# Masks ahead of sums, statistics in other slots, and the last decodes on VectorE, in a pre-norm graph-attention kernel

## The chip, the cores and the metric

The kernel runs on one core of a Trainium2 chip. A core has five engines that run at the same time, each working through its own queue in order: TensorE (PE in the profile; its weight loads are listed apart as PEld) multiplies matrices into PSUM, VectorE (DVE), ScalarE (ACT) and GpSimd (POOL) work element by element, and SyncE (SP) issues the transfers between memory and the on-chip SBUF. In this kernel POOL works from SBUF to SBUF only. An engine waits on semaphores that other engines raise, and whatever stands behind a waiting instruction in the same queue waits too.

The metric is the time of one execution in device microseconds; less is better. The median of three runs of the kernel before is 2755.74 us (2753.53 to 2756.32).

## The reference

The input x has 128 graphs of 128 nodes with 768 features, and adj has a 128 x 128 matrix for each graph. All is float32. For every graph:

```python
h = maximum(layernorm(x), 0)
q, k, v = (split_heads(h @ W + b) for W, b in ((Wq, bq), (Wk, bk), (Wv, bv)))   # 12 heads of 64
scores = q @ k.T / sqrt(64) + beta * adj
scores = where(adj > 0, scores, -9e15)
out = x + merge_heads(softmax(scores) @ v)
```

The three projections (768 x 768 each) are most of the arithmetic.

## The kernel before

**Groups and slices.** The 128 graphs go in 32 groups (G = 0 to 31) of 4. A group's projections are three slices: `qk0` (queries and keys of heads 0 to 5), `v` (all values) and `qk1` (queries and keys of heads 6 to 11). Each slice multiplies a 512 x 768 block of activations by weights. Group 0 does this plainly (`plain_slice`) and meanwhile VectorE and POOL prepare sums of weight blocks (`prepare`, lines 281 to 304), which are stored to memory. From group 1 on a fast scheme takes 15 block products in place of 18 (table `PRODUCTS`), and each block product is again split, into 7 small ones in place of 8. Both need sums: of activations, made by VectorE once per group (`sum_acts`, line 454, names S0 to S14) and by POOL (`inner`, lines 459 to 461), and of weights, streamed in again for every group through a ring of five buffers (`load_T`, line 335), except for eleven that stay in SBUF.

**Slots.** A slice from group 1 on is 15 slots, numbered 0 to 14, in the order that the tables `ZORDER` (qk0 and v), `QORDER` (qk1) or `LORDER` (qk1 of the last group) give. One slot is one product: 14 matmuls on line 537 into a PSUM bank pair, then work on the other engines. `run` and `behind_product` emit each slot in this order: the matmuls and the load of a later weight tile; then the steps listed for the slot; then the masks pending from earlier scores; then whatever has fallen due (`overdue`); then the copies of the product out of PSUM; then the queued exponentials and divisions (`trail`); and last the steps listed as "post" of the slot. Since each engine works in order, this is the order in every engine's queue. `then(at, f, ...)` puts a step in a slot, `then((at, "post"), f, ...)` behind it.

**Copies and decodes.** A product belongs to one of four chains (a, b, c, d). The first product of a chain takes a bank pair, further ones add to it, and the last gives it back. After each product the parts are added to their place: ScalarE copies where it is the first for that place (lines 552, 555, 557), VectorE adds otherwise (line 561). When a place has all its parts, `decode` turns the seven sums into queries and keys (lines 577 to 580) or values (588 to 592), one slot later or as `LAG` says, on POOL; only the decode behind product 13 of `qk1` is on VectorE. There are four bank pairs. From slot 2 to slot 9 of `qk0` the chains a, b and c hold three, and one is left for scores and attention.

**Attention.** For each pair of heads `scores` (line 614) multiplies keys and queries into a bank pair, `mask` (line 622, VectorE) adds the adjacency bias, writes to SBUF and gives the bank back, ScalarE takes the exponential (line 624), `attend` multiplies with the values (line 671, interleaved with the next product), ScalarE copies the result out (lines 680, 682) and divides (line 654) and VectorE adds x (line 696). The scores of `qk1`'s heads come in the next group's `qk0`, in slots 3, 5 and behind slot 6, so that their masks fall in slots 4, 6 and 7, and their attention behind slots 7, 10 and 12. In the last slice of the last group half steps are used (`scores_half`, lines 719 and 724; `attend_half`, lines 740 to 767).

**Statistics.** The layer normalisation of a later group is prepared by row: `load_row` (line 402) loads one graph's 128 x 768 block into the one place `row_home`, and `row_stats` (lines 409 to 411, ScalarE) takes its sum and its squared deviations, three instructions and two accumulator reads. As there is one place, the load of the next graph waits in SP's queue until the statistics before it are done. `row_moments` (line 416, then POOL 421 and 422, then two small transfers on lines 427 and 428) turns four graphs' statistics into the block layout in which `norm` (line 438, ScalarE) applies them to x, loaded by `load_x` (line 189). `to_hT` (line 449) transposes. In groups G with `G + 2 < NG` (NG = 32, so up to group 29) the statistics are those of group G + 2; group 1 does in addition those of group 2, as the fast scheme begins there.

Since group 30 has no group two after it, it runs `qk0` without statistics.

Of the kernel before, what the change touches and what calls it, by code (L numbers as in the profile page):

```python
# [125 lines left out]
def direct(ctx, tc, x, adj, wq, bq, wk, bk, wv, bv, beta, out, bad):  # L126
# [196 lines left out]
    def order_of(G, sl):  # L323
        return LORDER if G == NG - 1 and sl == "qk1" else ORDER[sl]
# [163 lines left out]
    def later(f, slots=1):  # L488
        while len(deferred) < slots:
            deferred.append([])  # L490
        deferred[slots - 1].append(f)
# [29 lines left out]
    def product_z(G, sl, n):  # L521

        an, bn, chain, uses = PRODUCTS[n]
        mine = [i for i in order_of(G, sl) if PRODUCTS[i][2] == chain]
        first = n == mine[0]
        if first:
            banks[chain] = take()
        p = banks[chain].rearrange("p i (z w) -> p (i z) w", w=P)
        a = full[G, an]
        streamed = (sl, n) not in resident  # L530
        b = tz.pop((G, sl, n)) if streamed else resident[sl, n]
        for at, z in enumerate(ZONES):
            lhs, rhs = a[:, LEFT[z]], b[:, RIGHT[z]]
            if sl != "v":
                lhs, rhs = rhs, lhs
            for q in range(0, P, HD):
                nc.tensor.matmul(p[q:q + HD, at, :], lhs[:, q:q + HD], rhs, start=(first and at % 4 == 0),  # L537
                                 stop=True, skip_group_check=True)
            turn()
        if streamed:  # L540
            load_T()
        yield
        for (r, j), sign in uses:
            key = (G, sl, r, j)
            op = ALU.add if sign > 0 else ALU.subtract
            if key not in qk:
                left[key] = sum(k == (r, j) for q in PRODUCTS for k, _ in q[3])
                t = qk[key] = home_qk(*key, zones=True)
                if sl == "v":
                    bias = bv_b[:, j * 2 * P:(j + 1) * 2 * P].rearrange("p (i n) -> p i n", i=2)  # L550
                    nc.vector.tensor_tensor(t[:, 5:7], bias, p[:, 5:7], op)
                    nc.scalar.activation(t[:, 0:5], p[:, 0:5], AF.Copy, scale=float(sign))
                else:
                    oc = j + 3 * int(sl[2])
                    nc.scalar.activation(t[:, 0:5], p[:, 0:5], AF.Copy, scale=float(sign))  # L555
                    for at, of in ((5, 0), (6, 2)):
                        nc.scalar.activation(t[:, at], p[:, at], AF.Identity, bias=bqk[:, of, oc:oc + 1],  # L557
                                             scale=float(sign))
            else:
                t = qk[key]  # L560
                nc.vector.tensor_tensor(t, t, p[:, 0:7], op)  # L561
            left[key] -= 1
            if not left[key]:
                later(lambda r=r, j=j: decode(G, sl, r, j, nc.vector if (sl, n) == ("qk1", 13) else nc.gpsimd), 1 if order_of(G, sl) is LORDER else LAG.get((sl, n), 1))
        if n == mine[-1]:
            give(banks.pop(chain))
        yield
# [205 lines left out]

    def behind_product(at, todo):
        pending = [masking.popleft() for _ in range(len(masking))]
        for f in todo.get(at, ()):
            f()
        for f in pending:
            f()
        while weighing:  # L780
            weighing.popleft()()
        overdue()
# [256 lines left out]
    for G in range(1, NG):  # L1039
# [6 lines left out]
        if G == 1:  # L1046
            sums_at(1, ((0, "S6"), (1, "S7"), (2, "S0"), (5, "S5"), (7, "S14"), (9, "S11")))
            then((0, "post"), load_x, 2, 0)
            for g, at in enumerate((2, 6, 10, 14)):
                then((at, "post"), row_stats, 2, g)  # L1050
                if g < 3:
                    then((at, "post"), load_row, 2, g + 1)
        else:
            sums_at(G, ((0, "S7"), (1, "S0"), (4, "S5"), (7, "S14"), (9, "S11")))
            if more:
                for g in range(2):
                    for h in range(2):
                        then((2 * g + h, "post"), norm, G + 1, g, 2 * h, 2 * h + 2)
                turn_act(G + 1, ((8, "A01"), (9, "A00"), (11, "A02")), None)
                then((12, "post"), load_x, G + 1, 1)  # L1060
                if G + 2 < NG:
                    then((8, "post"), row_stats, G + 2, 0)
                    then((9, "post"), load_row, G + 2, 1)
        slice_z(G, "qk0", todo)

# [4 lines left out]
        if more:  # L1070
            then((11, "post"), add_raw, G + 1)
            if G == 1:
                then(1, row_moments, 2, 3, 4)
                for n, at in enumerate((6, 7, 8, 9)):
                    then((at, "post"), norm, 2, n // 2, n % 2 * 2, n % 2 * 2 + 2)
                turn_act(2, ((10, "A01"), (11, "A00"), (12, "A02")), 1)
                then((12, "post"), load_x, 2, 1)
            else:
                for n, at in enumerate((3, 4, 7, 8)):
                    then((at, "post"), norm, G + 1, 2 + n // 2, n % 2 * 2, n % 2 * 2 + 2)  # L1080
                turn_act(G + 1, ((10, "A11"),), 1)
                for at, name in ((4, "A01"), (5, "A00"), (6, "A02")):
                    then(at, inner, G + 1, name)
            if G + 2 < NG:
                if G == 1:
                    then((1, "post"), load_row, 3, 0)
                for g, at in ((0, 5), (1, 11)) if G == 1 else ((1, 1), (2, 5), (3, 10)):
                    then((at, "post"), row_stats, G + 2, g)
                    if g < 3:
                        then((at + 1, "post"), load_row, G + 2, g + 1)  # L1090
        slice_z(G, "v", todo)

        todo.clear()
# [2 lines left out]
        attention(G, 0, ((3, 2), (9, 1)))  # L1096
        attention(G, 0, ((12, 0),), 6)
        if G == 1:
            for n, at in enumerate((0, 1, 2, 3)):
                then((at, "post"), norm, 2, 2 + n // 2, n % 2 * 2, n % 2 * 2 + 2)  # L1100
            turn_act(2, ((4, "A10"), (5, "A11"), (6, "A12")), 1)
            then((5, "post"), row_stats, 3, 2)
            then((5, "post"), load_row, 3, 3)
            then((9, "post"), row_stats, 3, 3)
        else:
            turn_act(G + 1, ((1, "A10"), (4, "A12")), 1)
        sums_at(G + 1, ((6 + (G == 1), "S1"), (7 + (G == 1), "S9"), (8 + (G == 1), "S2"), (11, "S6"), (13, "S10")))
        bias(G + 1, 0, 2, 4)
        if G + 2 < NG:
            then(*((10, row_moments, G + 2, 3, 5) if G == 1 else (5, row_moments, G + 2, 6, 9)))  # L1110
            then((6, "post"), load_x, G + 2, 0)
        if G + 3 < NG:
            then((10, "post"), load_row, G + 3, 0)
        slice_z(G, "qk1", todo)
# [151 lines left out]
```

## Time and profile before

| | |
|---|---|
| median of 3 runs | 2755.74 us (2753.53 to 2756.32) |
| profiled execution | 2751.8 us, its span 2749.9 us |
| mean granted clock of TensorE | 0.997 |
| one steady group (1339.20 to 1422.50) | 83.3 us: PE busy 81.75, DVE 67.86, ACT 55.79, POOL 65.81 |
| memory traffic in that group | 267 GB/s, the DMA engines busy 0.88 of the time |

The rows of the order of time show start, length, engine, line, operation, tiles written and read, and in brackets the idle time of that engine just before, with what ended it. Matmul ends are modelled, so a busy TensorE is not a TensorE at its peak. A row of the list of waits reads: who waited, for whom, microseconds in total, times, longest. "issue" is time in which an engine waited for nothing that the profile shows.

### The profile page before, as it was taken

What the parts mean: (1) busy time and instruction counts of PE and PEld (TensorE: products, weight loads), DVE (VectorE), ACT (ScalarE), POOL (GpSimd) and SP (SyncE); (2) the same over time, 40 slices, a digit from 0 to 9 for tenths busy, and PEclk for the clock granted to TensorE, in tenths of its full rate; (3) what the DMA queues carried; (4) which work ended last, traced back from release to release, by engine and by line L of the source; (5) the groups of instructions that cost most, each with busy time, mean ns of one, the idle gap of its engine ahead of it and who ended that gap; (6) DMA issues with size and microseconds to landing.
All of it is one profiled execution on the core that took longest, in us unless ns stands there. A gap on an engine that the chain in (4) does not pass through costs nothing.

```text
span 2749.9 us, 121542 instructions
## 1 busy us (share of the span) xinstructions
PE 2671.3 (97%) x52029; PEld 2565.2 (93%) x52029; DVE 2194.7 (80%) x2693; ACT 1763.8 (64%) x4612; POOL 2107.5 (77%) x3046
## 2 busy tenths in 40 slices
PE   9999999999999999999999999999999999999997
PEld 7688999999999999999999999999999999999997
DVE  6867887788887788887788887778877888877885
ACT  1377666666666766666676666766667666667653
POOL 4757878777788778787778787777887787877784
PEclk9999999999999999999999999999999999999999
DMA  8788889898889898898898898988888988998875
GB/s 209 246 269 266 269 263 280 252 280 268 266 274 272 254 277 266 270 274 265 270 271 266 264 282 252 279 268 263 273 272 259 275 265 271 273 262 272 254 235 153
DMA packets 530342, 721.73 MB, mean 262 GB/s; under 512 B 105980, under 2 KB 374024, under 8 KB 529800
## 3 DMA queue, kind: packets, MB, share of 16 engines
q1 hardware_dynamic: 528640, 713.12, 85.5%
q8 instruction: 412, 6.75, 1.0%
q10 hardware_dynamic: 1160, 0.79, 0.1%
q14 instruction: 130, 1.06, 0.1%
HBM read 647.73 MB, written 66.05 MB: 260 GB/s over the span
## 4 chain that ended last, share of the span: by engine, by line
PE 61%; DVE 16%; DMA 6%; ACT 6%; POOL 5%; issue 3%; SPq 0%; DVEq 0%; POOLq 0%; ACTq 0%
PE pair L537 51%; PE pair L614 5%; DVE home L561 5%; PE pair L671 5%; DVE sbig L454 5%; DMA turned<-row 2%; DMA T_qk<-kept_qk 2%; DVE e L622 2%; DVE xo L696 2%; ACT sbig L411 1%; ACT sbig L409 1%; DMA sbig<-in_x_dram 1%; DVE sbig L561 1%; ACT home L555 1%; ACT home L557 1%
## 5 line engine op out<-in xcount | busy, mean ns | idle before, releaser
L561 DVE TENSOR_TENSOR home<-home,pair 128x896 f32<-128x896 f32 x810 | 861.0, 1076 | 284.7 <-PE pair L537 187.2
L537 PE MATMUL pair<-sbig,T_qk 128*64 128x128 f32 x13888 | 886.1, 274 | 3.3 <-ACT home L557 2.2
L537 PEld LDWEIGHTS pair<-sbig,T_qk 128*64 128x64 f32 x13888 | 754.7, 137 | 16.8 <-ACT home L557 7.6
L654 ACT ACTIVATE e<-e,sm 128x64 f32<-128x64 f32 x1512 | 382.2, 342 | 108.2 <-DVE sm L642 108.0
L671 PE MATMUL pair<-v,e 128*64 128x65 f32 x6048 | 401.5, 222 | 27.4 <-ACT home L557 18.6
L577 POOL TENSOR_TENSOR home<-home 128x256 f32<-128x256 f32 x299 | 228.8, 765 | 259.1 <-DVE home L561 249.5
L537 PE MATMUL pair<-A,T_qk 128*64 128x128 f32 x6076 | 414.6, 273 | 0.0
L537 PE MATMUL pair<-T_v,sbig 128*64 128x128 f32 x6944 | 412.3, 273 | 0.0
L555 ACT ACTIVATE home<-pair 128x640 f32<-128x640 f32 x325 | 228.6, 703 | 263.5 <-PE pair L537 202.9
L671 PEld LDWEIGHTS pair<-v,e 128*64 128x64 f32 x6048 | 356.0, 137 | 38.6 <-ACT home L557 24.1
L537 PEld LDWEIGHTS pair<-T_v,sbig 128*64 128x64 f32 x6944 | 383.7, 137 | 5.5 <-issue 5.2
L537 PEld LDWEIGHTS pair<-A,T_qk 128*64 128x64 f32 x6076 | 330.1, 137 | 5.5 <-issue 5.5
L580 POOL TENSOR_TENSOR home<-home 128x256 f32<-128x256 f32 x299 | 280.3, 938 | 23.5
L622 DVE SCALAR_TENSOR_TENSOR e<-pair,biasT 128x1024 f32<-128x1024 f32 x189 | 230.5, 1220 | 35.4 <-PE pair L614 35.4
L578 POOL TENSOR_TENSOR home<-home 128x256 f32<-128x256 f32 x299 | 238.5, 798 | 23.4
L680 ACT ACTIVATE sm<-pair,tiny 128x8 f32<-128x8 f32 x189 | 50.4, 267 | 312.0 <-PE pair L671 311.9
L624 ACT ACTIVATE e<-e 128x1024 f32<-128x1024 f32 x189 | 200.1, 1059 | 64.6 <-DVE e L622 47.9
L579 POOL TENSOR_TENSOR home<-home 128x128 f32<-128x128 f32 x299 | 216.4, 724 | 23.4
L438 ACT ACTIVATE x<-x,block 128x192 f32<-128x192 f32 x480 | 231.2, 538 | 4.4 <-DMA block<-turned 3.0
L537 PE MATMUL pair<-sbig,res_qk 128*64 128x128 f32 x3472 | 211.6, 273 | 0.5 <-DVE home L561 0.5
L614 PE MATMUL pair<-home 64*64 64x128 f32 x5312 | 187.8, 275 | 18.1 <-DVE e L622 18.1
L557 ACT ACTIVATE home<-pair,bqk 128x128 f32<-128x128 f32 x650 | 203.3, 373 | 0.0
(188 smaller groups left out, 4702.9 us busy)
## 6 DMA issues: line engine op xcount, KB each, us to landing
T_qk<-kept_qk SPq DMA_DIRECT2D x713, 448.0 KB, 4.8
T_v<-kept_v SPq DMA_DIRECT2D x341, 448.0 KB, 4.3
xo<-in_x_dram SPq DMA_DIRECT2D x189, 256.0 KB, 4.9
out_dram<-xo SPq DMA_DIRECT2D x189, 256.0 KB, 5.9
x<-in_x_dram SPq DMA_DIRECT2D x248, 192.0 KB, 6.2
sbig<-in_x_dram SPq DMA_DIRECT2D x120, 384.0 KB, 6.5
kept_qk<-prep_qk SPq DMA_DIRECT2D x23, 448.0 KB, 3.2
adj<-in_adj_dram SPq DMA_DIRECT2D x128, 64.0 KB, 3.4
```

Of the source, the lines that this page charges most:

```text
L438: nc.scalar.activation(t, t, AF.Relu, bias=shift[G, n], scale=rstd[G, n])
L537: nc.tensor.matmul(p[q:q + HD, at, :], lhs[:, q:q + HD], rhs, start=(first and at % 4 == 0), stop=True, skip_group_check=True)
L555: nc.scalar.activation(t[:, 0:5], p[:, 0:5], AF.Copy, scale=float(sign))
L557: nc.scalar.activation(t[:, at], p[:, at], AF.Identity, bias=bqk[:, of, oc:oc + 1], scale=float(sign))
L561: nc.vector.tensor_tensor(t, t, p[:, 0:7], op)
L577: e.tensor_tensor(t[:, 1:4:2], t[:, 1:4:2], twice(5), ALU.add)
L578: e.tensor_tensor(t[:, 2:5:2], t[:, 2:5:2], twice(1), ALU.add)
L580: e.tensor_tensor(t[:, 0:7:6], t[:, 0:7:6], twice(2), ALU.add)
L614: nc.tensor.matmul(ps[k:k + HD, i, g * N:(g + 1) * N], keys[r, k:k + HD], queries[r], start=True, stop=True)
L622: nc.vector.scalar_tensor_tensor(e, ps, SCORE_CAP * ISCALE, bias, op0=ALU.min, op1=ALU.add)
L654: nc.scalar.activation(o[:, r, b, 0:HD], pa[:, r, b, 0:HD], AF.Copy, scale=t[:, 1, r, b:b + 1])
L671: nc.tensor.matmul(pa[q:q + HD, 2 * g + i, :], k[:, q:q + HD], vt[G, "v", r, h // 4][:, 4 * g + h % 4, :], start=True, stop=True, skip_gro ...
```

## The change

Four edits:

1. `behind_product` runs the pending masks ahead of the slot's steps instead of behind them. Where a slot has both, the mask comes before the sums, transposes or weight sums of that slot in VectorE's queue. In `qk0` of the steady groups this is slot 4 (S5) and slot 7 (S14).
2. From group 2 on the statistics of the first row of group G + 2 move from behind slot 8 to behind slot 7 of `qk0`. The load of the next row stays behind slot 9.
3. In group 1 the loads and statistics of group 3's rows come earlier: the first load behind slot 14 of `qk0`, statistics behind slots 2, 5 and 13 of `v` and slot 7 of `qk1`. The first normalisation of the second half of group 2 moves behind slot 14 of `v`, the others behind slots 0, 3 and 4 of `qk1`; transposes, sums, bias steps, `row_moments` and `load_x` in that slice shift accordingly.
4. In the last group's `qk1` the decodes behind products 11, 12 and 14 go to VectorE too.

```diff
-                later(lambda r=r, j=j: decode(G, sl, r, j, nc.vector if (sl, n) == ("qk1", 13) else nc.gpsimd), 1 if order_of(G, sl) is LORDER else LAG.get((sl, n), 1))
+                last = order_of(G, sl) is LORDER
+                engine = nc.vector if sl == "qk1" and (n == 13 or last and n in (11, 12, 14)) else nc.gpsimd
+                later(lambda r=r, j=j, engine=engine: decode(G, sl, r, j, engine), 1 if last else LAG.get((sl, n), 1))
...
     def behind_product(at, todo):
         pending = [masking.popleft() for _ in range(len(masking))]
+        for f in pending:
+            f()
         for f in todo.get(at, ()):
-            f()
-        for f in pending:
             f()
...
             for g, at in enumerate((2, 6, 10, 14)):
                 then((at, "post"), row_stats, 2, g)
-                if g < 3:
-                    then((at, "post"), load_row, 2, g + 1)
+                then((at, "post"), load_row, *((2, g + 1) if g < 3 else (3, 0)))
...
-                    then((8, "post"), row_stats, G + 2, 0)
+                    then((7, "post"), row_stats, G + 2, 0)
                     then((9, "post"), load_row, G + 2, 1)
...
-                if G == 1:
-                    then((1, "post"), load_row, 3, 0)
-                for g, at in ((0, 5), (1, 11)) if G == 1 else ((1, 1), (2, 5), (3, 10)):
+                for g, at in ((0, 2), (1, 5), (2, 13)) if G == 1 else ((1, 1), (2, 5), (3, 10)):
                     then((at, "post"), row_stats, G + 2, g)
                     if g < 3:
                         then((at + 1, "post"), load_row, G + 2, g + 1)
+                if G == 1:
+                    then((14, "post"), norm, 2, 2, 0, 2)
...
         if G == 1:
-            for n, at in enumerate((0, 1, 2, 3)):
+            for n, at in ((1, 0), (2, 3), (3, 4)):
                 then((at, "post"), norm, 2, 2 + n // 2, n % 2 * 2, n % 2 * 2 + 2)
-            turn_act(2, ((4, "A10"), (5, "A11"), (6, "A12")), 1)
-            then((5, "post"), row_stats, 3, 2)
-            then((5, "post"), load_row, 3, 3)
-            then((9, "post"), row_stats, 3, 3)
+            turn_act(2, ((5, "A10"), (6, "A11"), (7, "A12")), 1)
+            then((7, "post"), row_stats, 3, 3)
...
-        sums_at(G + 1, ((6 + (G == 1), "S1"), (7 + (G == 1), "S9"), (8 + (G == 1), "S2"), (11, "S6"), (13, "S10")))
-        bias(G + 1, 0, 2, 4)
+        sums_at(G + 1, ((6 + 2 * (G == 1), "S1"), (7 + 2 * (G == 1), "S9"), (8 + 2 * (G == 1), "S2"), (11, "S6"), (13, "S10")))
+        bias(G + 1, *((0, 7, 10) if G == 1 else (0, 2, 4)))
         if G + 2 < NG:
-            then(*((10, row_moments, G + 2, 3, 5) if G == 1 else (5, row_moments, G + 2, 6, 9)))
-            then((6, "post"), load_x, G + 2, 0)
+            then(*((8, row_moments, G + 2, 3, 5) if G == 1 else (5, row_moments, G + 2, 6, 9)))
+            then((8 if G == 1 else 6, "post"), load_x, G + 2, 0)
```

## The prediction

> **What bounds the kernel now.** I read the page first, then the list of TensorE's waits, then the order of time of one steady group (the one from 1389 to 1422 us, group 16), engine by engine.
>
> ```profile
> span 2749.9 us, 121542 instructions
> PE 2671.3 (97%) x52029; PEld 2565.2 (93%) x52029; DVE 2194.7 (80%) x2693; ACT 1763.8 (64%) x4612; POOL 2107.5 (77%) x3046
> ...
> PE pair L614 <- DVE e L622: 21.6, 30, 1.4
> PE pair L671 <- ACT home L557: 18.6, 23, 0.8
> ```
>
> TensorE is the bound: it idles 78.6 us of 2749.9, and 40.2 of those (21.6 + 18.6) are two waits that come back once in nearly every group. The other engines are busy 64 to 80%, so they matter only where TensorE waits for them. The sum below is made against this execution's own time, 2751.8 us (span 2749.9). The median of the runs, 2755.74, is 3.9 above it.
>
> **First row's statistics one slot earlier (groups 2 to 29: 28 times).** The second wait first. Columns: start, length, engine, line, operation.
>
> ```profile
> 1406.67 2.27 ACT L624 ACTIVATE e<-e 128x1024 f32<-128x1024 f32 x2
> 1410.69 0.27 ACT L680 ACTIVATE sm<-pair,tiny 128x8 f32<-128x8 f32 x1 [1.75 <-PE pair L671]
> 1410.85 0.59 ACT L682 COPY e<-pair 128x520 f32<-128x520 f32 x1
> 1411.33 0.85 ACT L409 ACTIVATE sbig<-sbig 128x768 f32<-128x768 f32 x1
> ...
> 1413.38 0.19 ACT L411 ACTIVATION_READ_ACCUMULATOR sbig<-sbig,strow 128x1 f32 x1
> 1414.06 0.61 ACT L557 ACTIVATE home<-pair,bqk 128x128 f32<-128x128 f32 x2
> ...
> 1410.47 1.70 PE L537 MATMUL pair<-sbig,T_qk 128*64 128x128 f32 x28
> 1412.00 1.70 PE L537 MATMUL pair<-A,T_qk 128*64 128x128 f32 x28
> 1414.72 0.45 PE L671 MATMUL pair<-v,e 128*64 128x65 f32 x8 [0.81 <-ACT home L557]
> ```
>
> The product that starts at 1410.47 (slot 9 of qk0, the last of its chain) ends at 1412.17. ScalarE must copy it out before its bank goes to the attention step in slot 11, but it is in the statistics (1411.33 to 1413.57), so the copy ends at 1414.67 and the attention step starts at 1414.72. Moved behind slot 7, the statistics fall where ScalarE idles 1.75 us, after the exponentials that end at 1408.94: 1408.9 to 1411.1. They push L680 and L682 back by 0.3 (they would end at 1411.74, and the product at 1412.00 takes that bank), and the copy can start with the product's end at 1412.2 and, as long as now (1413.57 to 1414.67), end at 1413.3, before the attention step needs the bank.
>
> The price can be read from the kernel itself: group 30 has no later group, so it runs the same slots without statistics. Start of slot 9 and of slot 12, group 29, then group 30:
>
> ```profile
> 2495.16 1.70 PE L537 MATMUL pair<-sbig,T_qk 128*64 128x128 f32 x28
> ...
> 2501.71 1.70 PE L537 MATMUL pair<-sbig,res_qk 128*64 128x128 f32 x28
> ...
> 2578.61 1.70 PE L537 MATMUL pair<-sbig,T_qk 128*64 128x128 f32 x28
> ...
> 2584.13 1.70 PE L537 MATMUL pair<-sbig,res_qk 128*64 128x128 f32 x28
> ```
>
> 6.55 us against 5.52: the statistics cost 1.03 us a group. 28 x 1.03 = 28.8 us gained. Bounds: 0 (another wait takes the place) and 28.8. I take all of it. SP gains with it: its load of the next row waits for the statistics, and that wait ends earlier.
>
> **Masks ahead of sums.** In slot 4 the sum S5 (L454) stands ahead of the mask (L622), which frees the only bank that the scores of slot 5 can take; in slot 7 S14 stands ahead of another mask.
>
> ```profile
> 1399.79 1.61 DVE L454 TENSOR_TENSOR sbig<-A,sbig 128x896 f32<-128x896 f32 x1
> ...
> 1404.99 1.33 DVE L454 TENSOR_TENSOR sbig<-sbig,A 128x896 f32<-128x896 f32 x1
> 1406.57 1.22 DVE L622 SCALAR_TENSOR_TENSOR e<-pair,biasT 128x1024 f32<-128x1024 f32 x1 [0.25 <-PE pair L614]
> 1408.33 1.09 DVE L561 TENSOR_TENSOR home<-home,pair 128x896 f32<-128x896 f32 x1 [0.54 <-PE pair L537]
> ...
> 1410.57 1.09 DVE L561 TENSOR_TENSOR sbig<-sbig,pair 128x896 f32<-128x896 f32 x1 [0.54 <-PE pair L537]
> ...
> 1402.68 1.10 PE L614 MATMUL pair<-home 64*64 64x128 f32 x32 [0.74 <-DVE e L622]
> 1405.40 1.10 PE L614 MATMUL pair<-home 64*64 64x128 f32 x32
> ...
> 1400.53 1.19 POOL L579 TENSOR_TENSOR home<-home 128x128 f32<-128x128 f32 x1
> ...
> 1404.11 0.46 POOL L579 TENSOR_TENSOR home<-home 128x128 f32<-128x128 f32 x1
> 1404.64 0.73 POOL L580 TENSOR_TENSOR home<-home 128x256 f32<-128x256 f32 x1
> ...
> 1411.65 1.61 POOL L580 TENSOR_TENSOR home<-home 128x256 f32<-128x256 f32 x1
> ```
>
> With the mask first it ends at 1399.79 + 1.22 = 1401.0 and the 0.74 us wait at 1402.68 goes. But I cost this at no gain, because of what is late next. The scores behind slot 6 (1405.40) need the keys that POOL decodes last; that decode ends at 1404.64 + 0.73 = 1405.37, at the moment TensorE arrives. A TensorE that is 0.74 early waits 0.74 there. So what counts is whether the swap moves POOL. Beside S5 POOL's L579 took 1.19 instead of 0.46 (0.73 lost). After the swap S5 runs from 1401.0 and meets POOL's next L580, which beside a sum took 1.61 instead of 0.73 (0.88 lost). POOL is then 0.15 later: 30 x 0.15 = 4.5 us lost. Bounds: 0.73 gained if S5 meets none of POOL's work, 0.88 lost if it holds a second operation too; I take 0.15 as both its rows are of this very pair.
>
> [...]
>
> In slot 7 the mask must wait for scores that end at 1406.5, and S14 now queues behind it: VectorE idles from 1404.99, where S14 starts now, to 1406.57, 1.6 us. S14 would end at 1406.57 + 1.22 + 1.33 = 1409.1 at the latest, and the next L561, which now starts at 1408.33, up to 0.8 late; the waits of 0.54 there and 0.54 at the L561 after it swallow that. S14 is multiplied in slot 11, behind the product that starts at 1412.00. I cost it at nothing; without those waits it is 1.6 a group.
>
> **The start.** Group 0's last slice has masks behind weight sums.
>
> ```profile
> 119.75 0.47 PE L671 MATMUL pair<-v,e 128*64 128x65 f32 x8 [3.52 <-DVE e L622]
> ...
> 127.54 1.33 DVE L454 TENSOR_TENSOR sbig<-A,A 128x896 f32<-128x896 f32 x1 [2.50 <-POOL A L461]
> ...
> 131.53 4.75 PE L537 MATMUL pair<-sbig,T_qk 128*64 128x128 f32 x84
> ```
>
> The 3.52 goes, but group 1 starts with S1, which is ready at 127.54 + 1.33 = 128.87 and waits for POOL. So at most 131.53 - 128.87 = 2.7 is gained, at least 0; I take 1.5.
>
> **Group 1's spread statistics.** Group 3's rows are now read within qk0 and v of group 1, each statistics step two or three slots behind its load in the first two cases.
>
> ```profile
> 166.94 0.33 SPq L402 DMA_DIRECT2D sbig<-in_x_dram  x1
> ...
> DMA to landing us min/median/max: 4.2/6.5/7.2
> ...
> 197.32 1.86 ACT L438 ACTIVATE x<-x,block 128x192 f32<-128x192 f32 x4 [1.36 <-DMA x<-in_x_dram]
> ...
> 209.81 1.97 PE L537 MATMUL pair<-sbig,T_qk 128*64 128x128 f32 x32 [1.97 <-ACT home L557]
> ```
>
> The load at 166.94 can't be earlier: it waits for the statistics before it. A load lands 4.2 to 7.2 after its issue, and two slots are 3.1 (a slot without scores or attention is 1.53, from 1410.47 to 1412.00): ScalarE waits up to 4 us at a row, with the copies of products queued behind it, and again at the next row. SP's queue stands still until the row is read, with the weight loads behind. The normalisation put behind v's last slot waits for x, which lands at 197.3, and the copies of qk1's first products, now ahead of it, stand behind it. Against that the 1.97 at 209.81 goes (the statistics that caused it are moved into v). Bounds: 2 gained, 8 lost (two waits of 4). The two sides meet in the middle of a slice in which later waits swallow part of a loss: I take 1.5 lost, nearer to the row that goes. The bias steps, transposes, sums and row_moments of that slice move by one to six slots; what they make is used a slice later: nothing.
>
> **The last decodes.** POOL's decode is in the chain at the end; VectorE's is shorter but stands in a queue.
>
> ```profile
> 2722.02 0.41 DVE L577 TENSOR_TENSOR home<-home 128x256 f32<-128x256 f32 x1
> ...
> 2723.25 0.43 DVE L580 TENSOR_TENSOR home<-home 128x256 f32<-128x256 f32 x1
> ...
> 2736.06 0.72 POOL L577 TENSOR_TENSOR home<-home 128x256 f32<-128x256 f32 x1 [1.60 <-DVE sm L757]
> ...
> 2737.44 0.29 DVE L767 TENSOR_TENSOR xo<-xo,o_last 128x128 f32<-128x128 f32 x1
> ...
> 2738.19 0.73 POOL L580 TENSOR_TENSOR home<-home 128x256 f32<-128x256 f32 x1
> ```
>
> VectorE needs 1.66 (2722.02 to 2723.68), POOL 2.86 (2736.06 to 2738.92). But POOL starts as soon as the product is added, while VectorE first does the last attention's division, up to L767's end at 2737.73: 2739.4, 0.5 later. The decode two slots before is late in the same way, by about 1. Bounds: 2 x 1.2 gained, 2.5 lost. I take 1.3 lost.
>
> **Sum.** -28.8 + 4.5 - 1.5 + 1.5 + 1.3 = -23.0. The profiled execution would take 2728.8, the median 2732.7: I say 2732.
>
> **Rivals.**
> A. The swap pays too: S5 falls where POOL has nothing to lose. Then 30 x 0.73 = 21.9 more instead of 4.5 less: 2706. Against it: POOL's additions follow one another without a gap there. 6 in 100.
> B. A new wait takes part of the gain: the statistics end too late for the bank of slot 10's product. I have it free at 1411.74 for a start at 1412.00; half a microsecond later costs 28 x 0.4 = 11 us: 2744. 13 in 100.
> C. Slower: VectorE loses 1.6 us in each group's slot 7 and does not make it up, 30 x 1.6 = 48 against the gain: 2781. It decides if VectorE's waits for products behind slot 7 (0.54, 0.54) were used up before a product needs a copy; it speaks against it that VectorE is 80% busy. 7 in 100.
> D. The change doesn't do what it says: S5 holds two of POOL's operations, 30 x 0.88 = 26 lost, which eats the 28.8: 2755. 4 in 100.
>
> **How the numbers follow.** My forecast has 70 in 100, with its own range 2720 to 2741 (the bounds of the start, of group 1 and of the end, +-0.15 a group for POOL). With most of B the range is 2716 to 2745. A measurement can tell 0.2%, 5.5 us, from no change: faster 0.89 (forecast, A, B), same 0.04, slower 0.07.
>
> **What would show it.** Right: no wait of L671 for L557 in groups 2 to 29; L409 right after the two L624 of slots 6 and 7; L614's wait for L622 gone and as large a wait for POOL's L580 behind slot 6; a steady group 0.9 us shorter. Wrong: a wait of L537 for L682 in slot 10 (B); scores behind slot 6 without a wait (A), or waiting more than 1.5 us (D); TensorE waiting for L561 from slot 8 on (C); over 8 us lost between 166 and 230 us.

## The result and the profile after

| | before | changed |
|---|---|---|
| median | 2755.26 us (2753.53 to 2756.32, 4 runs) | 2726.55 us (2724.22 to 2736.25, 4 runs) |
| profiled execution | 2751.8, span 2749.9 | 2724.2, span 2722.4 |
| mean granted clock of TensorE | 0.997 | 0.997 |

The ratio is 0.9903, with a 95% interval of 0.9878 to 0.9929: the change is worth 1.0%, 29 us. The forecast was 2732. Below, most of its terms turn out to be of another size, and two of the errors cancel.

In the changed kernel the lines from 565 to about 1050 have moved down by two: L614 is L616, L622 is L624, L671 is L673, L577 to L580 are L579 to L582, L654 is L656, L680 and L682 are L682 and L684.

The page of the changed kernel, its first two lines:

```profile
span 2722.4 us, 121562 instructions
PE 2674.2 (98%) x52029; PEld 2564.9 (94%) x52029; DVE 2192.7 (81%) x2705; ACT 1766.1 (65%) x4612; POOL 2093.6 (77%) x3034
```

TensorE idles 48.2 us (2722.4 - 2674.2), against 78.6 before. The list of its waits (who waited, for whom, us in total, times, longest):

```profile
PE pair L721 <- DVE home L581: 6.7, 2, 3.4
PE pair L537 <- ACT home L557: 5.6, 5, 3.8
PE pair L537 <- DVE e L624: 3.2, 9, 0.5
PE pair L616 <- issue: 3.1, 4, 1.7
```

The two waits that came back in nearly every group, 21.6 us for the mask and 18.6 us for the copy, are both gone. What leads the list now happens once (L721 is in the last slice, the 3.8 is in group 1) or at odd places.

One steady group, group 16, in order of time:

```profile
1389.97 1.10 PE L616 MATMUL pair<-home 64*64 64x128 f32 x32
...
1392.68 1.35 PE L616 MATMUL pair<-home 64*64 64x128 f32 x32
...
1398.00 1.70 PE L537 MATMUL pair<-sbig,T_qk 128*64 128x128 f32 x28
1399.53 1.70 PE L537 MATMUL pair<-A,T_qk 128*64 128x128 f32 x28
...
1403.52 1.70 PE L537 MATMUL pair<-sbig,res_qk 128*64 128x128 f32 x28
...
1387.87 1.21 DVE L624 SCALAR_TENSOR_TENSOR e<-pair,biasT 128x1024 f32<-128x1024 f32 x1
1389.01 1.08 DVE L454 TENSOR_TENSOR sbig<-A,sbig 128x896 f32<-128x896 f32 x1
...
1394.10 1.23 DVE L624 SCALAR_TENSOR_TENSOR e<-pair,biasT 128x1024 f32<-128x1024 f32 x1 [1.69 <-PE pair L616]
...
1396.38 0.83 ACT L409 ACTIVATE sbig<-sbig 128x768 f32<-128x768 f32 x1
...
1398.66 0.58 ACT L684 COPY e<-pair 128x520 f32<-128x520 f32 x1
...
1388.62 0.46 POOL L581 TENSOR_TENSOR home<-home 128x128 f32<-128x128 f32 x1
1389.16 1.52 POOL L582 TENSOR_TENSOR home<-home 128x256 f32<-128x256 f32 x1
...
1392.80 0.73 POOL L582 TENSOR_TENSOR home<-home 128x256 f32<-128x256 f32 x1
```

The mask (1387.87) now stands ahead of S5 (1389.01), and the scores of slot 5 (1389.97) start without a wait. From slot 9 to slot 12 it is 1403.52 - 1398.00 = 5.52 us, to the hundredth what group 30 took without statistics. The scores behind slot 6 (1392.68) begin without a wait too; the row is only 0.25 longer than an undisturbed one (1.35 against 1.10).

**Where the time went.** TensorE does the same matmuls in the same order in both kernels, so its times can be compared at the same work. Four stretches are used below: the start, to the first product of group 1; group 1, from there to slot 9 of group 2; the 27 steady groups from there to slot 9 of group 29; and the end. The rows that mark them, in order of time, before (its other two marks, 131.53 and 2495.16, stand in the prediction):

```profile
242.09 1.70 PE L537 MATMUL pair<-sbig,T_qk 128*64 128x128 f32 x28
```

and in the changed kernel:

```profile
125.23 3.28 PE L537 MATMUL pair<-sbig,T_qk 128*64 128x128 f32 x56 [1.38 <-issue]
...
244.80 1.70 PE L537 MATMUL pair<-sbig,T_qk 128*64 128x128 f32 x28
...
2468.39 1.70 PE L537 MATMUL pair<-sbig,T_qk 128*64 128x128 f32 x28
```

| us | start | group 1 | 27 groups | end |
|---|---|---|---|---|
| before | 131.5 | 110.6 | 2253.1 | 254.8 |
| changed | 125.2 | 119.6 | 2223.6 | 254.1 |
| difference | -6.3 | +9.0 | -29.5 | -0.7 |

The sum is -27.5, the difference of the spans. The gain is in the steady groups, 1.09 us in each; group 1 gives back more than the start wins.

### The profile page after: what moved, and what is told of

Same layout as the page of the kernel before. It is cut to its first block, busy times and chain, and to the rows that moved or that the text cites. A ratio compares the mean times of both kernels' runs of the same rounds, so it can differ in the third digit from the quotient of the medians.

```text
span 2722.4 us, 121562 instructions
## 1 busy us (share of the span) xinstructions
PE 2674.2 (98%) x52029; PEld 2564.9 (94%) x52029; DVE 2192.7 (81%) x2705; ACT 1766.1 (65%) x4612; POOL 2093.6 (77%) x3034
## 4 chain that ended last, share of the span: by engine, by line
PE 77%; DVE 6%; DMA 4%; ACT 4%; POOL 4%; issue 2%; SPq 1%; POOLq 0%; DVEq 0%; ACTq 0%
PE pair L537 66%; PE pair L616 6%; PE pair L673 5%; DVE home L561 2%; DMA sbig<-in_x_dram 2%; DMA x<-in_x_dram 1%; DMA T_qk<-kept_qk 1%; DVE sbig L454 1%; POOL home L579 1%; ACT sbig L411 1%; POOL home L580 1%; ACT e L656 1%; DVE e L624 1%; ACT sbig L409 1%; POOL home L582 1%
## 5 line engine op out<-in xcount | busy, mean ns | idle before, releaser
L561 DVE TENSOR_TENSOR home<-home,pair 128x896 f32<-128x896 f32 x810 | 860.0, 1076 | 237.0 <-PE pair L537 129.2
L537 PE MATMUL pair<-sbig,T_qk 128*64 128x128 f32 x13888 | 886.4, 273 | 5.5 <-DMA T_qk<-kept_qk 1.9
L537 PEld LDWEIGHTS pair<-sbig,T_qk 128*64 128x64 f32 x13888 | 754.4, 137 | 20.6 <-issue 8.7
L656 ACT ACTIVATE e<-e,sm 128x64 f32<-128x64 f32 x1512 | 383.2, 342 | 134.4 <-DVE sm L644 134.3
L579 POOL TENSOR_TENSOR home<-home 128x256 f32<-128x256 f32 x297 | 229.0, 771 | 242.5 <-DVE home L561 237.4
L537 PE MATMUL pair<-A,T_qk 128*64 128x128 f32 x6076 | 414.7, 273 | 0.2 <-DVE sbig L561 0.2
L537 PE MATMUL pair<-T_v,sbig 128*64 128x128 f32 x6944 | 412.6, 273 | 0.9 <-ACT home L552 0.8
L673 PE MATMUL pair<-v,e 128*64 128x65 f32 x6048 | 399.6, 221 | 1.3 <-ACT e L684 1.3
L537 PEld LDWEIGHTS pair<-T_v,sbig 128*64 128x64 f32 x6944 | 383.6, 137 | 7.0 <-issue 5.0
L673 PEld LDWEIGHTS pair<-v,e 128*64 128x64 f32 x6048 | 357.1, 137 | 4.9 <-ACT e L684 1.6
L537 PEld LDWEIGHTS pair<-A,T_qk 128*64 128x64 f32 x6076 | 330.0, 137 | 5.9 <-issue 5.3
L582 POOL TENSOR_TENSOR home<-home 128x256 f32<-128x256 f32 x297 | 277.2, 933 | 23.3
L624 DVE SCALAR_TENSOR_TENSOR e<-pair,biasT 128x1024 f32<-128x1024 f32 x189 | 230.4, 1219 | 75.4 <-PE pair L616 75.0
L580 POOL TENSOR_TENSOR home<-home 128x256 f32<-128x256 f32 x297 | 246.5, 830 | 23.3
L581 POOL TENSOR_TENSOR home<-home 128x128 f32<-128x128 f32 x297 | 199.8, 673 | 23.3
L682 ACT ACTIVATE sm<-pair,tiny 128x8 f32<-128x8 f32 x189 | 49.6, 262 | 254.7 <-PE pair L673 254.7
L537 PE MATMUL pair<-sbig,res_qk 128*64 128x128 f32 x3472 | 211.7, 273 | 0.5 <-DVE sbig L454 0.5
L557 ACT ACTIVATE home<-pair,bqk 128x128 f32<-128x128 f32 x650 | 204.6, 376 | 0.0
L616 PE MATMUL pair<-home 64*64 64x128 f32 x5312 | 196.0, 277 | 5.2 <-issue 3.1
```

The source lines that it names most:

```text
L579: e.tensor_tensor(t[:, 1:4:2], t[:, 1:4:2], twice(5), ALU.add)
L580: e.tensor_tensor(t[:, 2:5:2], t[:, 2:5:2], twice(1), ALU.add)
L582: e.tensor_tensor(t[:, 0:7:6], t[:, 0:7:6], twice(2), ALU.add)
L616: nc.tensor.matmul(ps[k:k + HD, i, g * N:(g + 1) * N], keys[r, k:k + HD], queries[r], start=True, stop=True)
L624: nc.vector.scalar_tensor_tensor(e, ps, SCORE_CAP * ISCALE, bias, op0=ALU.min, op1=ALU.add)
L656: nc.scalar.activation(o[:, r, b, 0:HD], pa[:, r, b, 0:HD], AF.Copy, scale=t[:, 1, r, b:b + 1])
```

## The experiments

The stretches of all runs, taken from the same rows of each trace, with ratios to the kernel before, measured beside it on the same chip:

| run | median, us | ratio (95%) | start | group 1 | 27 groups | end |
|---|---|---|---|---|---|---|
| e1_stats | 2730.55 | 0.9920 (0.9907 to 0.9932) | 131.0 | 110.9 | 2232.4 | 253.2 |
| e2_masks | 2739.12 | 0.9946 (0.9934 to 0.9958) | 128.1 | 112.6 | 2244.5 | 252.0 |
| e3_no_spread | 2718.63 | 0.9872 (0.9856 to 0.9887) | 126.8 | 112.4 | 2225.5 | 253.7 |
| e4_pool_last | 2730.16 | 0.9918 (0.9904 to 0.9931) | 127.1 | 119.0 | 2222.4 | 251.6 |
| e5_rows_turned | 2743.64 | 0.9956 (0.9939 to 0.9972) | 128.9 | 120.5 | 2236.2 | 254.7 |
| e6_norm_back | 2725.92 | 0.9891 (0.9870 to 0.9912) | 128.4 | 115.7 | 2228.4 | 254.2 |
| e7_two_edits | 2716.90 | 0.9869 (0.9849 to 0.9888) | 127.1 | 112.9 | 2220.8 | 251.4 |
| e8_row2_later | 2714.98 | 0.9855 (0.9838 to 0.9871) | 126.0 | 112.9 | 2215.7 | 252.9 |
| e9_turns_back | 2723.94 | 0.9888 (0.9871 to 0.9905) | 129.4 | 115.4 | 2223.3 | 254.8 |
| e10_half_sent | 2708.44 | 0.9836 (0.9822 to 0.9851) | 124.7 | 115.7 | 2215.1 | 251.2 |
| e11_rows_early | 2717.36 | 0.9875 (0.9858 to 0.9892) | 126.0 | 116.6 | 2214.7 | 252.8 |
| e12_changed_row2 | 2724.28 | 0.9894 (0.9875 to 0.9913) | 128.3 | 119.8 | 2220.6 | 253.9 |

A stretch is of one profiled execution, and that was up to 8.2 us faster than its run's median (e4_pool_last; 5.8 in e8_row2_later, 5.5 in e11_rows_early). So a difference of some 5 us in the 27 groups between two rows can be scatter.

### The two edits of the steady groups, each alone

e1_stats is the kernel before with

```diff
-                    then((8, "post"), row_stats, G + 2, 0)
+                    then((7, "post"), row_stats, G + 2, 0)
```

> The kernel before with one edit: the first row's statistics of groups 2 to 29 stand behind slot 7 of qk0 instead of slot 8. As on record: 28 x 1.03 = 28.8 us gained, 2726. By the trace of the changed kernel, where TensorE gains 0.93 to 0.98 at the attention step behind slot 9: 26 to 27.4 gained, 2728. If the moved statistics pay only because the masks moved too: under 10 gained.

e2_masks is the kernel before with

```diff
+        for f in pending:
+            f()
         for f in todo.get(at, ()):
-            f()
-        for f in pending:
             f()
```

> The kernel before with one edit: masks ahead of the slot's other steps. As on record: 4.5 us lost in the groups and 1.5 gained at the start, 2758. By the trace of the changed kernel: the scores of slot 5 start 0.8 earlier and only 0.2 comes back behind slot 6, 30 x 0.6 = 18 gained and 4.6 at the start, of which scattered waits elsewhere may take up to 10: 2733 to 2743. The attention step behind slot 9 still waits 0.8 for the copy (L557).

The waits of TensorE in e1_stats, and then those in e2_masks (same columns; both keep the line numbers of the kernel before):

```profile
PE pair L614 <- DVE e L622: 18.6, 28, 0.8
PE pair L537 <- DVE home L561: 3.8, 5, 1.0
PE pair L614 <- issue: 3.5, 6, 1.1
```

```profile
PE pair L671 <- ACT home L557: 18.6, 23, 0.8
PE pair L671 <- ACT sbig L557: 4.0, 5, 0.8
```

Each edit takes away its own wait and leaves the other nearly as it was (18.6 of 21.6 us for the mask in e1_stats, 18.6 of 18.6 for the copy in e2_masks). Together, in e7_two_edits below, they gain what both gain alone (a ratio of 0.9869 against 0.9920 x 0.9946 = 0.9866), so the two are independent. The statistics alone gain 22.0 us on the median (2752.53 - 2730.55), 20.7 of them in the 27 groups, less than either reading had told, and do not need the masks to move. From slot 9 to slot 12 each of the 27 groups takes 5.52 us or 0.01 less, against 6.55 before: at this place the 1.03 arrives in full, and what is missing is lost elsewhere. The masks alone gain 13.4, with 8.6 in the 27 groups: not a loss of 4.5. Matmul by matmul, an otherwise undisturbed group of e2_masks is 0.6 us shorter than the same group before: 0.81 gained at the scores of slot 5, 0.2 lost behind slot 6.

### Why the masks pay: which scores need the last decode

The profile lists the scores of one pair of heads as 32 records, 8 for each of four graphs. A decode writes the places of the seven sums in four steps (L579 to L582 in the changed kernel); the last step writes sums 0 and 6, and the kernel reads those only for the second graph of a row pair:

```python
        return t[:, (3, 4, 0, 6)[2 * g + i], :]
```

So of the scores behind slot 6 only the last graph, the last 8 of 32 records, needs the last step of POOL's last decode. e5_rows_turned takes the two row pairs the other way round there:

```diff
-        for g in range(GRP):
+        for g in ((2, 3, 0, 1) if (u, j) == (1, 1) else range(GRP)):
```

> The changed kernel; the scores behind slot 6 take their row pairs in the other order, so that their first half, not their second, needs the keys that POOL decodes last. If the scores behind slot 6 gave back only 0.2 us a group because just their second half (0.5 us in) needs that decode: now they wait 0.7 at their start, 30 x 0.5 = 15 us slower than the changed kernel, 2741. If the scores need all keys at their start, as on record: no change, 2726.

The scores behind slot 6 of group 16 in this run, and POOL's last decode ahead of them:

```profile
1400.39 0.45 PE L616 MATMUL pair<-home 64*64 64x128 f32 x8
1401.19 0.89 PE L616 MATMUL pair<-home 64*64 64x128 f32 x24 [0.36 <-POOL home L582]
...
1400.41 0.73 POOL L582 TENSOR_TENSOR home<-home 128x256 f32<-128x256 f32 x1
```

The first 8 records run, then TensorE stands until L582 ends (1401.14): the needed graph is now the second of four. The ratio is 0.9956 against 0.9903 for the changed kernel, 15 us slower, with 12.6 of them in the 27 groups. (The expectation says that the second half needs the decode; it is the last quarter.) In the changed kernel's own group 16 the last 8 records are these:

```profile
1393.58 0.45 PE L616 MATMUL pair<-home 64*64 64x128 f32 x8
```

In the undisturbed scores of slot 5 the last 8 begin 0.71 us behind the first record. Here that would be 1393.39, when L582 has 0.14 to go (1392.80 + 0.73 = 1393.53), so they begin 0.2 late, as the longer row said. In the kernel before they began at 1406.10, and the decode was done at 1405.37: TensorE had 0.7 us in hand there.

### Group 1's spread

e3_no_spread is the changed kernel with edit 3 undone. e6_norm_back undoes one piece of it,

```diff
-                if G == 1:
-                    then((14, "post"), norm, 2, 2, 0, 2)
...
-            for n, at in ((1, 0), (2, 3), (3, 4)):
+            for n, at in enumerate((0, 1, 2, 3)):
```

e9_turns_back undoes that and also

```diff
-            turn_act(2, ((5, "A10"), (6, "A11"), (7, "A12")), 1)
+            turn_act(2, ((4, "A10"), (5, "A11"), (6, "A12")), 1)
```

> The changed kernel with group 1's spread undone (group 3's rows, the normalisations and the steps of qk1 stand where they stood before). As on record the spread lost 1.5: 2725. By the trace of the changed kernel group 1 lost 7 us against the kernel before, and if all of that is the spread: 2719.5. If it is the earlier arrival that meets the same loads: 2726.5, no change.

> The changed kernel with one piece of group 1's spread undone: the first normalisation of the second half of x stands in qk1's slot 0 again, not behind v's last slot. If ScalarE's 9.1 us wait for x ahead of the first copies of qk1 is what group 1 loses: the 3.8 us wait of TensorE behind qk1's slot 2 goes, 4 us faster than the changed kernel, 2722. If the late x and the late rows are the cause wherever the normalisation stands: under 1.5 faster.

> The changed kernel with two pieces of group 1's spread undone: the normalisation as in e6_norm_back, and the transposes of qk1 in slots 4 to 6 instead of 5 to 7. The rows' spread, the sums and the bias steps stay as changed. If what is left of group 1's loss comes from POOL's queue (the second of its steps on the transposed blocks stands behind a product's decode, so the first sum waits 7 us and TensorE 4.7 behind it): that wait falls to 1 and the kernel is 4 to 6 us faster than the changed one, 2721. If the late x alone decides: as e6_norm_back, 2726.

Group 1 of the changed kernel in order of time:

```profile
187.96 2.92 SPq L189 DMA_DIRECT2D x<-in_x_dram  x4
...
194.24 0.98 ACT L438 ACTIVATE x<-x,block 128x192 f32<-128x192 f32 x2 [9.14 <-DMA x<-in_x_dram]
...
197.49 3.19 PE L537 MATMUL pair<-A,res_qk 128*64 128x128 f32 x28 [3.82 <-ACT home L557]
...
213.34 1.60 DVE L454 TENSOR_TENSOR sbig<-A,A 128x896 f32<-128x896 f32 x1 [3.73 <-POOL A L461]
...
216.92 2.69 PE L537 MATMUL pair<-A,res_qk 128*64 128x128 f32 x28 [2.68 <-DVE home L561]
```

The normalisation behind v's last slot stands 9.14 us for x, whose loads SP issues from 187.96 on. The copies of the first products of qk1 stand behind it, and TensorE waits 3.82. Later the first sum waits for POOL's steps on the transposed blocks, VectorE's addition L561 stands behind that sum, and TensorE waits 2.68. Behind each of these two waits the granted clock is 0.50 for 3.4 us (from 197.1 and from 217.6), which costs at most 1.7 each (half of the 3.4); the kernel before has no such stretch in group 1 (its granted clock is 1.00 from 131.6 to 242.0).

e3_no_spread came out at 2718.63, a ratio of 0.9872 against 0.9903: without the spread the kernel is some 8 us faster. Group 1 takes 112.4 to 112.9 us without it (e2, e3, e7, e8; only e10, whose transfers differ, took 115.7), with all of it 119.0 to 120.5 (changed, e4, e5, e12): 7.0 on the means. With the normalisation back it is 115.7, so that piece costs 4, one of the two stretches at half clock included. But the total of e6_norm_back shows little of it (0.9891 against 0.9903, overlapping), since its steady stretch was 4.8 longer, which is of the size of the scatter. In its order of time the 3.82 is gone, and the sum waits longer:

```profile
212.60 1.59 DVE L454 TENSOR_TENSOR sbig<-A,A 128x896 f32<-128x896 f32 x1 [6.99 <-POOL A L461]
...
216.18 3.25 PE L537 MATMUL pair<-A,res_qk 128*64 128x128 f32 x28 [4.65 <-DVE home L561]
```

I took POOL's order for the cause: the second of its steps on the transposed blocks (L459 to L461) came behind a product's decode. e9_turns_back put it ahead of the decode, and that theory fell: TensorE's wait at this place shrank from 4.65 to 2.4, not to 1, and the stretch stayed at 115.4, although the half clock behind the wait was gone too, while other waits grew (over the whole run those for L552 from 1.8 to 2.3, those for L561 on sbig from 1.7 to 2.5). In both runs POOL works there almost without a gap (its rows show no idle time from 199 to 214 in e6_norm_back and from 197 to 219 in e9_turns_back), so all of its queue is late, whatever its order. What is left is the rows' part, which e11_rows_early has by itself (e8_row2_later plus the early loads and statistics of group 3's rows):

```diff
-                if g < 3:
-                    then((at, "post"), load_row, 2, g + 1)
+                then((at, "post"), load_row, *((2, g + 1) if g < 3 else (3, 0)))
...
-                if G == 1:
-                    then((1, "post"), load_row, 3, 0)
-                for g, at in ((0, 5), (1, 11)) if G == 1 else ((1, 1), (2, 6), (3, 11)):
+                for g, at in ((0, 2), (1, 5), (2, 13)) if G == 1 else ((1, 1), (2, 6), (3, 11)):
...
-            then((5, "post"), row_stats, 3, 2)
-            then((5, "post"), load_row, 3, 3)
-            then((9, "post"), row_stats, 3, 3)
+            then((7, "post"), row_stats, 3, 3)
```

> The kernel of e8_row2_later with the rows' part of group 1's spread and nothing else of it (the normalisation, transposes, sums and bias steps stay as before the change). If the rows' early statistics pay by themselves (the 1.8 us wait for the copy behind qk1's slot 8 goes): 1 to 2 us faster than e8_row2_later, 2713. If ScalarE's waits for rows that have not landed cost as much: no change, 2715.

Its ScalarE in v of group 1:

```profile
169.27 0.85 ACT L409 ACTIVATE sbig<-sbig 128x768 f32<-128x768 f32 x1 [1.84 <-DMA sbig<-in_x_dram]
...
175.68 0.84 ACT L409 ACTIVATE sbig<-sbig 128x768 f32<-128x768 f32 x1 [2.05 <-DMA sbig<-in_x_dram]
```

Both statistics come before their row has landed. The copies behind them are late, the decodes of v with them, and the first sum of the next group again waits for POOL (4.74). The stretch is 116.6 against 112.9 in e8_row2_later: the rows' part costs 3.7, with one stretch at half clock (from 213.5) that e8_row2_later does not have. So the spread's 7 us are the normalisation's 4 and the rows' 3 to 4.

### The last decodes

e4_pool_last is the changed kernel with edit 4 undone.

> The changed kernel with the last decodes back on POOL. As on record the move to VectorE lost 1.3: 2725. By the trace of the changed kernel TensorE's two waits at the end grew by 1.4 and 1.2 us, but its products ran 2 us faster behind them: 2724 if the full clock stays without the longer waits, 2726.5 (no change) if the half clock comes back with the shorter ones.

TensorE's wait at the end in that run, which answers to the 6.7 of the changed kernel:

```profile
PE pair L719 <- POOL home L579: 3.5, 2, 1.9
```

The medians don't separate the two (0.9918 against 0.9903, overlapping intervals). The end does: 251.2 to 253.2, on the mean 252.2, in the seven experiments with POOL's decodes, and 253.7 to 254.8, mean 254.2, in the six runs with VectorE's. The move costs about 2. The kernel before (254.8) hides this, for two reasons. From slot 9 of group 29 to slot 9 of group 30 it lacks the gain of the first two edits (83.5 us against 81.5 to 82.6 in the runs with both). And it had two stretches at half clock in its last slice: from slot 9 of group 30 on it took 171.3, as did e11_rows_early with two such stretches at the same places, while e4_pool_last took 169.3 without one. The busy times of each engine there, with TensorE's granted clock as the third figure from the end of each row, before, and then in e4_pool_last:

```profile
2731.40:2734.60 3.20, 3.20 (x36) 2.97 (x30) 0.81 (x2) 0.63 (x1) 2.63 (x4) 0.50 0.58 166
2738.20:2741.40 3.20, 3.10 (x49) 2.37 (x50) 1.36 (x6) 1.40 (x3) 0.72 (x1) 0.50 0.44 123
```

```profile
2703.00:2706.20 3.20, 2.86 (x60) 2.49 (x60) 2.14 (x3) 1.08 (x2) 2.41 (x5) 1.00 0.76 210
2708.70:2711.90 3.20, 2.34 (x60) 1.79 (x62) 1.44 (x6) 1.67 (x5) 0.73 (x1) 1.00 0.38 108
```

### What gives part of the gain back

e7_two_edits is the kernel before with the edits of e1_stats and e2_masks together. An undisturbed group gains 1.03 by the one and 0.57 by the other (0.81 less 0.24), 43 us in 27 groups; the stretch is 32.3 shorter, so 11 us come back. TensorE's waits over 0.1 us that are new or left there are 7 us, against 1.3 in the kernel before (all for the mask in v): 5 that the list puts down to "issue", 0.8 for the mask in v, 0.8 that the list puts down to a decode. Matmul by matmul against the kernel before, 8.2 of the 11 are lost at one place: in the scores of one pair of heads in v, where most of the "issue" waits stand, and the wait put down to a decode too (the decode had ended 0.57 earlier). In the changed kernel 7.1 are lost there; it waits also 1.9 for weights, and 2.7 for the mask in v. The wait for the mask can be followed back in the changed kernel's order of time:

```profile
929.23 0.85 ACT L409 ACTIVATE sbig<-sbig 128x768 f32<-128x768 f32 x1 [1.49 <-DMA sbig<-in_x_dram]
...
932.09 1.09 DVE L561 TENSOR_TENSOR sbig<-sbig,pair 128x896 f32<-128x896 f32 x1 [3.79 <-ACT sbig L552]
933.09 1.22 DVE L624 SCALAR_TENSOR_TENSOR e<-pair,biasT 128x1024 f32<-128x1024 f32 x1
...
934.36 1.75 PE L537 MATMUL pair<-res_v,A 128*64 128x128 f32 x28 [0.51 <-DVE e L624]
```

ScalarE reaches the statistics of the third row in v before the row has landed, the copy of a product (L552) stands behind them, VectorE's addition waits for the copy, the mask stands behind the addition, and TensorE waits for the mask's bank. e8_row2_later (on e7_two_edits) and e12_changed_row2 (on the changed kernel) give that row one slot more:

```diff
-                ... ((1, 1), (2, 5), (3, 10)):
+                ... ((1, 1), (2, 6), (3, 11)):
```

e10_half_sent is e7_two_edits without the output transfers of the odd pairs of heads.

> The kernel before with two edits: masks first, and the first row's statistics one slot earlier; group 1's spread and the last decodes by VectorE are left out. As on record (-28.8 + 4.5 - 1.5): 2727 on this scale. By the runs so far (statistics 22, masks 13, less up to 2 that the two share; the last decodes lost 2 in the changed kernel): 2717, faster than the changed kernel by 9.

> The kernel of the two edits, with the third row's statistics one slot later in v (behind slot 6 instead of 5) and the fourth row's load and statistics after it. If part of the gain is given back because ScalarE now reaches this row before it has landed, and the copies and the mask behind it are late (TensorE's waits for the mask in v, 3 us in all): these waits go, 2 to 3 us faster than the two edits alone. If they come from elsewhere: no change.

> The changed kernel with one edit: the third and fourth row's statistics of groups 3 to 31 one slot later in v. Between slot 9 of group 2 and slot 9 of group 29 the changed kernel and its relatives took 2221 to 2228 us, e8_row2_later and e11_rows_early 2215 to 2216. If that difference comes from the rows' place in v: 2215 here too, no wait of TensorE for the mask in v, and 2719 to 2722 as a whole. If it was chance: 2221 to 2228, and 2726.

> The kernel of the two edits that leaves out half of its output transfers (the odd heads' columns of every group but the last parts; 33 of 66 MB written), so half of the output is missing. If the scattered waits of the faster kernel (TensorE for its instructions in the scores of v, for weights, for the mask behind a late row: 7 us in all) come from transfers that wait for one another: most of them go, 4 to 7 us faster than the two edits alone, 2711. If they have another cause: no change, 2717.

e7_two_edits came out at 2716.90, as expected from e1 and e2, some 9 us under the changed kernel, though the two intervals still overlap. In e8 and e12 no wait of L537 for the mask in v is left in the 27 groups (0.8 us in e7, 2.7 in the changed kernel), so that chain is shown. What it is worth the stretches don't show: e12's was 2220.6, not 2215, because the "issue" waits grew. Matmul by matmul, e12 gains 4.4 us on the changed kernel around the products behind that mask and 4.1 behind slot 6, where the 0.24 a group is no longer lost (why, is not shown), and loses some 7.5 in the scores of v, a stretch at half clock (from 2239.1) included; e8 gains 2.0 and 4.4 on e7 at the same two places. TensorE's waits in e12_changed_row2:

```profile
PE pair L616 <- issue: 7.7, 9, 1.8
```

In the changed kernel that was 3.1. For each of the 11 "issue" waits over 0.2 us behind 300 us in the changed kernel, e1 and e2, a transfer of 16 KB on the instruction queue had begun 2.4 to 2.9 us before it ended. And from group to group the place of those in the scores of v moves on evenly: counted from slot 9 of qk0 they stand at matmul 364 in group 9, 367 in group 14 and 373 in group 26 of the changed kernel, at 361, 368 and 373 in groups 3, 17 and 26 of e7. So I take them for late instructions; that is a reading of these figures, and the profile names no releaser. Their total differs from trace to trace. e10 moved 24.6 MB less (721.7 to 697.1; the expectation's 33 was too many) and its stretch was 5.7 shorter than e7's, yet 2.9 us of "issue" waits in the scores remained of 3.6. That transfers hold one another up is suggested by this, not shown, since 5.7 is of the size of the scatter; why a given wait comes stays open.

e8_row2_later has the lowest median of the complete kernels, 2714.98, a ratio of 0.9855 (0.9838 to 0.9871). It isn't separated from e7_two_edits, but its interval lies below that of the changed kernel: it is faster than both kernels of this case.

## Why the prediction was nearly right, and where it was not

**Statistics (-28.8): right in the mechanism and in the price.** L673 no longer waits for L557 in the steady groups, L409 follows the exponentials of slots 6 and 7, and the bank of slot 10 is free at 1399.24 (1398.66 + 0.58) for a product at 1399.53, so rival B did not come. Group 30 gave the price, 1.03, and every steady group of e1_stats gains it at that place. On the whole kernel 22 of the 28.8 arrive: in the 27 groups 7 come back, 5.8 of them in the scores of v, at the "issue" waits. "I take all of it" left no room for that.

**Masks (+4.5): wrong. Alone they gain 13.4, of which 8.6 in the 27 groups.** The step that failed is "The scores behind slot 6 (1405.40) need the keys that POOL decodes last", taken as needing them at their start. Only their last quarter does. So the sign that was named for this term, as large a wait behind slot 6 as the one that went, did not come, and the sign of rival A, scores there without a wait, did. The rest of the step held. S5 left L581 (0.46 now, where L579 took 1.19) and met L582 (1.52, where I had put 1.61). By the row alone POOL's last decode would end 0.15 later against TensorE's unhindered course; from 1389.97 to 1393.53 it is 3.56, before it was 1405.37 - 1402.68 + 0.74 = 3.43, so 0.13 later. In slot 7 VectorE idles 1.69 for the mask (I had 1.6) and makes it up, so rival C did not come. Rival A has the outcome, by another mechanism: POOL did lose, and it did not matter.

**Start (-1.5): about right, by two errors.** The start is 4.1 us shorter in the runs with masks first (127.2 on the mean of twelve against 131.2 for the two without), more than the bound of 2.7, and group 1 then takes 2.0 longer without any spread (112.7 against 110.7; why, is not shown). The bound took the first sum as fixed at 127.54. In the changed kernel it starts at 123.80, since POOL's steps ahead of it come earlier too (their last begins at 123.31, before at 127.06). The 3.4 us at half clock that followed the wait of 3.52 before (from 120.1) are gone as well.

**Group 1 (+1.5): mis-sized, +7.0.** The chain named was right: the rows, the x that lands late, the copies behind it. The bound of 8 held; the choice near its lower side, "later waits swallow part of a loss", did not. And "what they make is used a slice later: nothing" failed: the first sum, behind the moved transposes and POOL's late steps, held VectorE up, and TensorE 2.68 us behind it, in the same slice.

**Last decodes (+1.3): mis-sized, +2.0,** the direction and the cause as told.

**Not in the sum: 11 us (e7) to 14 us (changed) of the 27 groups' gain that come back,** in "issue" waits above all, and for weights and a row's transfer. In the trace of before only the mask in v stood, with 1.3.

Against the terms, the 27 groups gained 29.5 where 27 x 0.88 = 23.8 was told: the masks gave 19 more than told (27 x 0.72), and 14 came back that were not told. The spread lost 5.5 more than told. These errors cancel, and the forecast of the whole was off by 5.5 only (2732 against 2726.55). That is luck; of the large terms only the price of the statistics was foreseen.

## What to carry to other kernels

When a wait is removed and you ask what is late next, read in the code which part of the waiting work needs the late piece: a run of 32 matmul records waits at the record that reads it, not at the first (0.36 us behind the first 8 in e5_rows_turned). Price a moved step against the landing of what it reads, since on an engine that works in order an early step that waits costs everything behind it (here ScalarE's 9.14 us for x put 3.82 on TensorE). And where the engines leave little room, expect some of a gain that comes back in every group to return as small waits at other places; here about a quarter did (11 of 43 us in e7_two_edits).

## What the runs showed of the hardware

- TensorE can stand in the middle of a run of matmuls with no releaser in the profile ("issue"): 1.69 us behind 25 of the 32 records of one pair of heads in the changed kernel (to 2238.72), up to 1.8 us at a time in these lists, in all 3.1 us in the scores of the changed kernel and 7.7 in e12_changed_row2, with none in the list of the kernel before. The profile of the changed kernel counts 412 transfers on the instruction queue and 4 of these waits in the scores.
- Of two waits of the same length one brought half clock behind it and the other did not. A wait of 1.91 us (to 2730.29) brought half clock in the last slice of the kernel before (0.50 from 2731.25), and the same wait of 1.91 (to 2702.49) none in e4_pool_last (1.00 from 2703.00 to 2706.20). In the changed kernel full clock lasted beyond a wait of 3.29 (to 2704.03):

```profile
2704.20:2707.40 3.20, 3.08 (x68) 2.52 (x63) 3.10 (x7) 0.63 (x1) 0.00 (x0) 1.00 0.52 151
```

  The stretches at half clock that end before the kernel does are each 3.41 us long in these two traces: from 10.83, 120.06, 2731.25 and 2738.08 in the kernel before, from 197.1 and 217.6 in the changed kernel. What decides whether one follows a wait is not shown. What this is worth in the last slice is of the size of edit 4's own 2 us (171.3 with two stretches, 169.3 without one).
